# A graph layer on one core: columns copied by ScalarE alone, for 110 tiles instead of 298, with the edge attributes split in portions

## The chip, the cores and the metric

The kernel runs on one core of a Trainium2 chip. The core has TensorE (PE, matrix products), VectorE (DVE), ScalarE (ACT), GpSimd (POOL), the queue of SyncE (SP), which issues most transfers here, and 16 DMA engines that carry them out. GpSimd issues the gathers: one indirect DMA fetches 128 rows of a table in HBM, one row for each partition. The metric is the device time of one execution in microseconds (us). "Span" is the time from the first to the last instruction of the profiled execution.

## The reference, cut to what matters

N = 12500 nodes with 96 features, E = 412500 edges sorted by their target, 4 attributes to an edge.

```python
def _mlp(h, W, b, gamma, beta):
    h = relu(h @ W + b)
    mu, var = mean(h, axis=0), var(h, axis=0)
    return gamma * (h - mu) * rsqrt(var + EPS) + beta

node_feat = _mlp(x, W_node, ...)
edge_feat = _mlp(edge_attr, W_edge, ...)
message = concatenate([x[row], x[col], edge_feat], axis=1)
message = _mlp(message, W_msg, ...)
agg = segment_sum(message, col, num_segments=N)
x = layernorm(x + agg + node_feat)
```

The message's product falls into three: x[row] @ W1 + x[col] @ W2 + edge_feat @ W3. The first two are tables over nodes.

## The kernel before

**Units.** An edge tile is 128 edges (3223 of them), a group is 4 tiles = 512 edges (806 groups, `NG`), a block is 4 groups (202 blocks, `NBL`). Since the edges are sorted by target, a block's targets lie in a window of 31 nodes for each group.

**Tables and gathers.** `tables` writes `p_tab` = x @ W1 and `q_tab` = x @ W2 to HBM. `gather(g, pg)` lets GpSimd fetch the rows of `p_tab` for the sources of a group's tiles, one indirect DMA to a tile (L214). The groups of the first 4 blocks (`RAW`) are gathered from the input x instead, before `p_tab` is there. GpSimd is in use from the beginning: the generator `blocks` gathers the first 29 blocks (116 groups, `SPILL`) into a ring of 8 pairs of groups and stores them to HBM (`spill`, L239 to L241, on SP's queue). Block b's gathers need the ring slots of block b - 4; the spill store of block b - 2 is issued at the step at which the gathers of block b are. Every `next(store)` in the setup is such a step. `early_rows` fetches the last tile of three of these groups row by row on SP instead.

**Setup.** After the tables come: the targets relative to their blocks (`rel`) and a check; `split`, which splits the edge attributes into three bf16 parts (8 steps of 128 x 1792 elements: load x, ScalarE copies to bf16, VectorE subtracts, twice over, three stores to `stack_d`); `places`, which does the like for the targets' places; and then `edge_norm`, the statistics of the edge features. `edge_norm` loads `stack_d` in chunks of J = 8 blocks by `stacked` (three DMAs), multiplies (L425), applies Relu (L429, ScalarE) and takes statistics (L431, VectorE, `bn_stats`, 606 of them); at its end it aggregates them (L436), sums over the partitions with the matrix `pick` and makes the `bias` and the weight `w_e`. Between its chunks it steps `nodes` (the node features, L370 to L406), `early_rows` and `store`; what is left of these is drained behind it, `nodes` first.

**Main loop.** SP, GpSimd, PE, DVE and ACT follow an order written out by hand (`manual_schedule`). It runs over the 806 groups in the order of `plan`, which mixes the 116 spilled groups in among the 690 others. For a step k with group g: `message(k)` (L740, VectorE) adds the gathered rows to the product in PSUM and applies Relu; `squared` (L754, ScalarE) and `moments` (L760, VectorE) collect the squares; `places_of` (L748) marks each edge's target in its window, `sums` (L786, PE) adds the messages by target, `add` (L805, L806) adds the window to `agg`; `edges` (L704) and `prepare` (L712, ScalarE) make the edge features of the next block in `left`; `linear` (L720) multiplies them and the window's rows of `q_tab` (in `rhs`) for the step after the next. For a group past the spilled ones, `ahead_of(ahead)` then issues the gathers of the group 16 places further on, into the ring slots that this pair of groups has freed.

**Copied tiles.** For certain pairs of groups the last tile isn't gathered. Instead its 128 source columns are copied from x, which lies transposed in SBUF (`big`), into a tile `xc` of 96 x 128, one column to an instruction, with the column's place in a register; PE then multiplies `xc` by W1 (L725). `COPIED` lists the pairs: nine out of ten, 298 in all. Two `Stream`s share them, ScalarE's (L647, 24 columns to a step) and VectorE's (L645, 25 to a step on the mean, in the portions of `LOADS`); `load` reads the places into registers, `copy` issues the copies. `listed` fetches the places from HBM on SP's queue. In a slot whose tile isn't gathered, `ahead_of` has the place zeroed by VectorE (L506) unless it is zero already.

```python
COPIED = [q for q in range(RING // 2, LP - 6) if q % 10 != 10 - 1]
...
    a, b = to[:, 4 * (lo + i):4 * (lo + i + 1)], places_in_x[:, bass.ds(x - HOME, 4)]
```

**End.** Behind the last step come the statistics of the messages and `output`, the normed sum for all nodes.

Of the kernel before, what the change touches and what calls it, by code (L numbers as in the profile page):

```python
# [26 lines left out]
P = 128  # L27
# [12 lines left out]
NS = 3  # L40
RW = 7
NBQ = RW * 32
RL = NBQ * GE
NPL = 8
PART = 4
# [69 lines left out]
def gnn(ctx, tc, t):  # L115
# [10 lines left out]
    stack_d = dram.tile([HI + PLACES * BG, RL], BF16, name="stack_d")  # L126
# [126 lines left out]

    zero = const.tile([64, C], F32, name="zero")
# [52 lines left out]
    def split():  # L307

        with tc.tile_pool(name="sp", bufs=2) as work:
            n = RL // 8 // NPL  # L310
            rows = [stack_d[16 * i:16 * (i + 1), :].rearrange("r (c e) -> (r c) e", c=8) for i in range(3)]
            ea = t["ea"].rearrange("r (c b) e -> (r c) (b e)", c=8)
            made = []
            for k in range(NPL + 1):
                if k < NPL:
                    x = work.tile([P, n], F32, name="x")
                    nc.sync.dma_start(x, ea[:, k * n:(k + 1) * n])
                    y = [work.tile([P, n], BF16, name=f"y{i}") for i in range(3)]
                    nc.scalar.activation(y[0], x, AF.Copy)
                    nc.vector.tensor_sub(x, x, y[0])  # L320
                    nc.scalar.activation(y[1], x, AF.Copy)
                    nc.vector.tensor_sub(y[2], x, y[1])
                    made.append(y)
                if k:
                    for i in range(3):
                        nc.sync.dma_start(rows[i][:, (k - 1) * n:k * n], made[k - 1][i])
                if k % 3 == 2:
                    yield

    def places():  # L330

        with tc.tile_pool(name="lin", bufs=2) as work, tc.tile_pool(name="lin1", bufs=1) as one:
            first = one.tile([P, RW], I32, name="first")
            nc.sync.dma_start(first, t["first"])
            rows = [stack_d[HI + BG * i:HI + BG * (i + 1), :].rearrange("g (c b e) -> (g c) b e", b=RW, e=GE)
                    for i in range(PLACES)]
            parts = [slice(i, min(i + 2, RW)) for i in range(0, RW, 2)]
            made = []
            for i in range(len(parts) + 1):
                if i < len(parts):  # L340
                    n = parts[i].stop - parts[i].start
                    lin = work.tile([P, n, GE], I32, name="lin")
                    nc.sync.dma_start(lin, t["dlin"][:, parts[i], :])
                    rlin = work.tile([P, n, GE], F32, name="rlin")
                    nc.vector.tensor_tensor(rlin, lin, first[:, parts[i]].unsqueeze(2).to_broadcast([P, n, GE]),
                                            op=OP.subtract)
                    y = [work.tile([P, n, GE], BF16, name=f"z{i}") for i in range(PLACES)]
                    nc.scalar.activation(y[0], rlin, AF.Copy)
                    nc.scalar.activation(rlin, rlin, AF.Square)
                    nc.scalar.activation(y[1], rlin, AF.Copy)  # L350
                    nc.vector.tensor_sub(y[2], rlin, y[1])
                    made.append(y)
                if i:
                    for r, x in zip(rows, made[i - 1]):
                        nc.sync.dma_start(r[:, parts[i - 1], :], x)

    def stacked(to, b, n):

        cols = slice(b * GE, (b + n) * GE)
        for lo, hi, rows in ((16, 48, 32), (0, 16, 16), (HI, ON, HI + PLACES * BG)):  # L360
            nc.sync.dma_start(to[lo:hi], stack_d[:rows, cols].rearrange("r (b e) -> r b e", e=GE))
# [46 lines left out]
    def edge_norm(work, one, ps):  # L408
# [5 lines left out]
        for b in range(NBL):  # L414
# [6 lines left out]
            for i in range(NS):  # L421
                k = NS * b + i
                if k % 2 == 0:
                    pr = ps.tile([P, 2, GE], F32, name="pr")
                nc.tensor.matmul(pr[:, k % 2, :], wide[:, P * i:P * (i + 1)], ea[:, b % J, :],  # L425
                                 start=True, stop=True)
                if k % 2:
                    r = work.tile([P, 2, GE], F32, name="r", bufs=4)
                    nc.scalar.activation(r, pr, AF.Relu)  # L429
                    for o in (1, 0):  # L430
                        nc.vector.bn_stats(stats[:, (k - o) % NS, (k - o) // NS, :], r[:, 1 - o, :])  # L431

        part = one.tile([P, NS, 2], F32, name="part")
        square = one.tile([P, NS], F32, name="square")
        for i in range(NS):
            nc.vector.bn_aggr(part[:, i, :], stats[:, i, :, :].rearrange("p a b -> p (a b)"))  # L436
        nc.vector.tensor_mul(square, part[:, :, 0], part[:, :, 0])
        nc.vector.tensor_add(part[:, :, 1], part[:, :, 1], square)
        pick = one.tile([P, NS, C], F32, name="pick")
        nc.vector.memset(pick, 0.0)  # L440
        for i in range(NS):
            for o in range(-P * i % C - C, P, C):
                lo, hi = max(o, 0), min(o + C, P)
                if lo < hi:
                    to = pick[:, i, lo - o:hi - o]
                    nc.vector.tensor_add(to, to, ident[:, lo:hi])
        pm = ps.tile([C, 2], F32, name="pr")
# [3 lines left out]
        nc.vector.tensor_scalar(aggr, pm, float(NBL * GE) / E, None, op0=OP.mult)  # L451
# [5 lines left out]
        pb = ps.tile([1, C], F32, name="pr")  # L457
# [39 lines left out]
    def fast():  # L497
# [14 lines left out]
        with tc.manual_schedule(engines={ET.SP, ET.Pool}):  # L512
# [9 lines left out]
            with tc.tile_pool(name="nd", bufs=1) as nd, tc.tile_pool(name="nd_ps", bufs=2, space=PSUM) as nd_ps, \  # L522
                    tc.tile_pool(name="er", bufs=2) as er, tc.tile_pool(name="es", bufs=2) as es, \
                    tc.tile_pool(name="es1", bufs=1) as es1, tc.tile_pool(name="es_ps", bufs=3, space=PSUM) as es_ps:
                node, n, extra = nodes(nd, nd_ps), 7, early_rows(er)
                for i, _ in enumerate(edge_norm(es, es1, es_ps)):
                    next(node, None)
                    if i:
                        next(extra, None)
                    while 16 * i + 150 >= 20 * n:  # L530
                        next(store, None)
                        n += 1
                for x in (node, store, extra):
                    for _ in x:
                        pass
            got = {g: ahead_of(g) for g in range(SPILL, SPILL + RING)}
        with tc.tile_pool(name="fix", bufs=1) as fix, tc.tile_pool(name="msg", bufs=2) as work, \
                tc.tile_pool(name="msg_ps", bufs=2, space=PSUM) as ps:
            squares = fix.tile([P, C], F32, name="squares")
# [5 lines left out]
            by_place = [ps.tile([P, GE], F32, name=f"pa{i}", bufs=1) for i in range(2)]  # L545
# [10 lines left out]
            for x in left:  # L556
                nc.vector.memset(x[C:], 1.0)
# [4 lines left out]
            at = [fix.tile([P, BG, OW], F32, name=f"at{i}") for i in range(AB)]  # L562
            for x in at:
                nc.vector.memset(x, 0.0)
# [8 lines left out]
            late = [fix.tile([P, CL, GE], BF16, name=f"late{i}") for i in range(2)]  # L573
            early = fix.tile([P, CE, GE], BF16, name="early")
            for x in (*late, early):
                nc.vector.memset(x[C:], 1.0)

            def load(s):
# [17 lines left out]
                nc.sync.dma_start(rhs[C:C + WN, s % RB, :, :], rows)  # L596
# [24 lines left out]
            loaded = []  # L621

# [16 lines left out]
            def columns(j, lo, val, engine):  # L639

                to = xcs[j % XB].bitcast(U8)
                for i, x in enumerate(val):
                    a, b = to[:, 4 * (lo + i):4 * (lo + i + 1)], places_in_x[:, bass.ds(x - HOME, 4)]
                    if engine == ET.DVE:
                        nc.vector.tensor_copy(a, b)  # L645
                    else:
                        nc.scalar.activation(a, b, AF.Copy)  # L647
# [59 lines left out]
            def prepare(s, half):  # L707

                n = min(2, NG - order[s] * BG - 2 * half)
                if n > 0:  # L710
                    pr, x = prs.pop((s, half)), left[s % 2]
                    nc.scalar.activation(x[:C + WN, 2 * half:2 * half + n, :], pr[:C + WN, :n, :], AF.Relu)  # L712
# [44 lines left out]
            def moments(sq, at_last, stream=None):  # L757

                for i in range(2):
                    nc.vector.tensor_tensor(wide_sq, wide_sq, sq[:, i, :, :], op=OP.add)  # L760
                    if stream:
                        stream.load()
# [48 lines left out]
            with tc.manual_schedule(engines={ET.SP, ET.Pool, ET.PE, ET.DVE, ET.Activation}):  # L811
# [9 lines left out]
                prepare(1, 0)  # L821
                for k in range(ZB - 1):
# [3 lines left out]
                for k in range(last):  # L826
# [9 lines left out]
                    dves.load()  # L836
# [324 lines left out]
```

## Time and profile before

| | |
|---|---|
| runs shown | 3755.09, 3759.74, 3773.7 us (median 3759.74) |
| profiled execution, its own time | 3756.5 us |
| its span | 3754.8 us |
| HBM read, written | 243.91 MB, 56.09 MB |
| setup, up to the first L740 | 0 to 683 us |
| main loop and end | 683 to 3754.8 us |

A line of the costliest groups reads: line, engine, operation, out<-in with shapes, count | busy us, mean ns of one | idle time of the engine just before them and what ended it. "issue" means that nothing in the profile had to be waited for. A timeline's row reads: start in us, length, engine, line, operation, out<-in, count [idle time before <- what ended it]. Times and rows come from one profiled execution. In the rows for TensorE an operation may be missing; the rows of GpSimd's gathers are complete (2922).

### The profile page before, as it was taken

The page shows a single profiled execution, that of the slowest core. Times are in us where ns is not written, and L with a number is a line of the kernel's source. Part 1 is how long each engine was busy: PE and PEld are TensorE (multiplying, and loading weights), DVE is VectorE, ACT ScalarE, POOL GpSimd, SP SyncE. Part 2 cuts the span into 40 slices and gives each one's busy share as a digit, 9 for nine tenths or more (in the row PEclk, how much of TensorE's full clock was granted, in tenths as well). Part 3 has the DMA queues.
Part 4 walks back from the last instruction along what each step waited for, and adds up shares of the span by engine and source line. Part 5 has one row for each costly group of instructions (what it writes and reads, how often), then busy time and mean ns, then how long its engine had stood idle before and what let it go on. Part 6 is the DMA issues. An engine that isn't in the chain of part 4 may idle for free.

```text
span 3754.8 us, 85646 instructions
## 1 busy us (share of the span) xinstructions
PE 2529.5 (67%) x15765; PEld 2135.2 (57%) x15765; DVE 3048.1 (81%) x22677; ACT 2903.9 (77%) x19786; POOL 2805.0 (75%) x2950
## 2 busy tenths in 40 slices
PE   4335664677776777667777767777766767776766
PEld 4012231576666666656766666666665666666666
DVE  2489999788888888888888888888888888888864
ACT  1457885588888888888888888888888888888852
POOL 7777775777777777777777777777777777777776
PEclk7667786788888877887787787887888787788776
DMA  8764663222222222222222222222222222222233
GB/s 236 261 178 111 164 171 99 65 63 60 58 62 61 57 66 49 60 62 59 59 63 61 61 62 58 61 62 58 61 62 51 63 59 60 61 58 65 58 100 74
DMA packets 206325, 305.80 MB, mean 81 GB/s; under 512 B 121814, under 2 KB 128708, under 8 KB 202944
## 3 DMA queue, kind: packets, MB, share of 16 engines
q0 software_dynamic: 93504, 143.81, 18.8%
q1 hardware_dynamic: 99308, 151.50, 13.5%
q10 hardware_dynamic: 12960, 4.93, 0.5%
q14 instruction: 427, 3.50, 0.3%
q8 instruction: 126, 2.06, 0.2%
HBM read 243.91 MB, written 56.09 MB: 80 GB/s over the span
## 4 chain that ended last, share of the span: by engine, by line
DVE 50%; DMA 14%; issue 12%; POOL 12%; DVEq 9%; PE 1%; ACT 1%; SPq 0%; ACTq 0%; POOLq 0%
DVE xc L645 25%; POOL pg L214 12%; DMA pg<-p_tab,src 11%; DVE estats L431 9%; DVEq L634 9%; DVE mixed L760 7%; DVE h L740 4%; DMA q_tab<-trow 1%; DVE agg L806 1%; DMA x<-in_ea 1%; DVE at L748 1%; PE pt L198 1%; DMA cols<-in_lasts 0%; DVE nstats L372 0%; DVE agg L381 0%
## 5 line engine op out<-in xcount | busy, mean ns | idle before, releaser
L214 POOL DMA_INDIRECT pg<-p_tab,src x2858 | 2722.5, 953 | 903.1 <-issue 720.8
L647 ACT ACTIVATE xc<-big 96x4 uint8 x18560 | 1846.9, 191 | 208.0 <-issue 201.6
L720 PE MATMUL z<-rhs,left 128*128 128x96 f32 x6446 | 1157.1, 335 | 847.4 <-DVE h L740 829.7
L645 DVE COPY xc<-big 96x4 uint8 x19584 | 1540.7, 195 | 226.7 <-issue 220.4
L720 PEld LDWEIGHTS z<-rhs,left 128*128 128x128 f32 x6446 | 1018.4, 240 | 947.5 <-DVE h L740 925.3
L786 PEld LDWEIGHTS pa<-at,h 128*97 128x97 f32 x6446 | 839.6, 207 | 117.5 <-issue 50.6
L786 PE MATMUL pa<-at,h 128*97 128x80 f32 x6446 | 848.6, 287 | 3.3 <-DVE h L740 3.3
L754 ACT ACTIVATE sq<-h 128x768 f32<-128x768 f32 x404 | 338.1, 837 | 287.5 <-DVE h L740 282.8
L740 DVE CUSTOM_DVE_ANT_0 h<-z,pg 128x384 f32<-128x384 f32 x690 | 374.5, 543 | 193.6 <-DMA pg<-p_tab,src 185.1
L760 DVE TENSOR_TENSOR mixed<-mixed,sq 128x384 f32<-128x384 f32 x802 | 448.6, 559 | 53.5 <-DVE h L740 18.4
L712 ACT ACTIVATE left<-pr 127x1024 f32<-127x1024 f32 x403 | 403.5, 1001 | 39.7 <-PE pr L704 39.7
L429 ACT ACTIVATE r<-pr 128x1024 f32<-128x1024 f32 x303 | 306.7, 1024 | 99.1 <-DVE estats L431 73.1
L425 PE MATMUL pr<-ea,wide 128*128 128x512 bf16 x606 | 225.2, 466 | 223.0 <-ACT r L429 146.8
L431 DVE BATCH_NORM_STATS2 estats<-r 128x6 f32<-128x512 f32 x606 | 361.0, 675 | 5.3 <-ACT r L429 5.3
L704 PE MATMUL pr<-late,we 128*128 128x512 bf16 x690 | 279.4, 497 | 17.7 <-DVE at L748 15.4
L425 PEld LDWEIGHTS <-wide 128*128 128x128 bf16 x606 | 67.4, 112 | 355.6 <-issue 257.6
L748 DVE TENSOR_TENSOR at<-rel,mixed 128x496 f32<-128x496 bf16 x202 | 132.3, 655 | 4.9 <-DVE h L740 4.6
L725 PE MATMUL z<-w_msg,xc 96*128 96x96 f32 x596 | 131.6, 307 | 0.0
L704 PEld LDWEIGHTS <-we 128*128 128x128 bf16 x806 | 109.6, 140 | 21.1 <-issue 19.5
L725 PEld LDWEIGHTS z<-w_msg,xc 96*128 96x128 f32 x596 | 107.1, 224 | 0.0
L805 DVE TENSOR_TENSOR total<-pa,total 97x1 f32<-97x1 f32 x202 | 31.8, 157 | 57.0 <-issue 45.8
L214 POOL DMA_INDIRECT pg<-in_x,src_raw x64 | 60.7, 949 | 20.6 <-issue 19.2
(132 smaller groups left out, 803.9 us busy)
## 6 DMA issues: line engine op xcount, KB each, us to landing
pg<-p_tab,src POOLq DMA_INDIRECT x2858
pb<-spill SPq DMA_DIRECT2D x29, 768.0 KB
spill<-pg SPq DMA_DIRECT2D x55, 384.0 KB
ea<-stack_d SPq DMA_DIRECT2D x25, 480.0 KB
stack_d<-y SPq DMA_DIRECT2D x24, 448.0 KB
late<-stack_d SPq DMA_DIRECT2D x57, 180.0 KB
rhs<-q_tab SPq DMA_DIRECT2D x202, 46.5 KB
x<-in_ea SPq DMA_DIRECT2D x8, 896.0 KB
```

The lines of the kernel that those rows point to most:

```text
L214: made = [nc.gpsimd.indirect_dma_start(out=pg[:, i, :], out_offset=None, in_=tab[:, :], in_offset=bass.IndirectOffsetOnAxis(ap=idx[:, i:i ...
L431: nc.vector.bn_stats(stats[:, (k - o) % NS, (k - o) // NS, :], r[:, 1 - o, :])
L634: _, val = nc.values_load_multi_w_load_instructions(numbers[q // TURN % 2][:, q % TURN, lo:hi], engines=[engine], min_val=HOME, max_val=HO ...
L645: nc.vector.tensor_copy(a, b)
L647: nc.scalar.activation(a, b, AF.Copy)
L704: nc.tensor.matmul(prs[s, half][:, i, :], we[:, 2 * half + i, :], block[s], start=True, stop=True)
L712: nc.scalar.activation(x[:C + WN, 2 * half:2 * half + n, :], pr[:C + WN, :n, :], AF.Relu)
L720: nc.tensor.matmul(zb[k % ZB][:, i * C:(i + 1) * C], left[s % 2][:KR, g % BG, i * P:(i + 1) * P], rhs[:KR, s % RB, g % BG, :], start=True, ...
L740: nc.vector._custom_dve(TENSOR_ADD_SAT, out=h[:, :n, :], in0=z, in1=rows[:, :n, :], s0=MOST, s1=0.0)
L754: nc.scalar.activation(sq[:, :m, :n, :], hb[k // 2 % HP][:, k % 2:k % 2 + m, :n, :C], AF.Square)
L760: nc.vector.tensor_tensor(wide_sq, wide_sq, sq[:, i, :, :], op=OP.add)
L786: nc.tensor.matmul(by_place[s % 2][:C + 1, :NW], hb[k // 2 % HP][:r, k % 2, t, :], at[s % AB][:r, i, o + NW * t:o + NW * (t + 1)], start=i ...
```

## The change

- `COPIED` lists every third pair (q % 3 == 1), 110 tiles, and `LOADS` gives all columns to ScalarE, 20 to a step; VectorE's stream is empty. The copy is of one f32 column rather than four bytes. (`columns` has a new form for VectorE, which isn't used with these `LOADS`.)
- `split` and `places` become one generator, `stacking`: 16 steps of 128 x 896 attributes, on every other step with one eighth of the places (112 x 512). `stack_d` is cut into 8 portions of 28 blocks. Four steps stand ahead of `edge_norm`, the others between its chunks, which are of 7 blocks now. The drain behind it takes `store` first and `nodes` last.
- `edge_norm` ends with sums over the statistics in place of L436 (a Square on ScalarE, three reductions and one more operation on VectorE); the rest of its end is `edge_bias`, called at the head of the main loop's section, behind first writes by ScalarE of the rows of ones and VectorE's zeroing of one `at`. `pick` is made earlier.
- The bias is written into `rhs` in one ScalarE instruction, at row C instead of the last row, in place of 12 DMAs; the weights in `wp` are turned to match, so that `prepare` covers all 128 rows and `left` needs no ones.
- In the main loop VectorE's places for reading registers are one in place of four.

```diff
-LOADS = (((24,),) * 4, ((8, 8, 12), (20,), (8, 8, 12), (12, 12)))
+LOADS = (((20,),) * 4, ((),) * 4)
-COPIED = [q for q in range(RING // 2, LP - 6) if q % 10 != 10 - 1]
+COPIED = [q for q in range(RING // 2, LP - 6) if q % 3 == 1]
-J = 8
+J = 7
-    stack_d = dram.tile([HI + PLACES * BG, RL], BF16, name="stack_d")
+    stack_d = [dram.tile([HI + PLACES * BG, PB * GE], BF16, name=f"stack{i}") for i in range(NPT)]
...
+    def stacking(one, work):
+        first = one.tile([BG * PB, NPT], I32, name="first")
+        nc.sync.dma_start(first, t["first"])
+        n = PB * GE // 8 // 2
+        made = []
+        def stored():
+            for to, x in made:
+                nc.sync.dma_start(to, x)
+            made.clear()
+        for u in range(2 * NPT):
+            p, half = u // 2, slice(u % 2 * n, (u % 2 + 1) * n)
+            x = work.tile([P, n], F32, name="x")
+            nc.sync.dma_start(x, t["ea_by_part"][p][:, half])
+            if u % 2 == 0:
+                lin = one.tile([BG * PB, GE], I32, name="lin")
+                nc.sync.dma_start(lin, t["dlin"][p])
+            stored()
+            y = [work.tile([P, n], BF16, name=f"y{i}") for i in range(3)]
+            nc.scalar.activation(y[0], x, AF.Copy)
+            nc.vector.tensor_sub(x, x, y[0])
+            nc.scalar.activation(y[1], x, AF.Copy)
+            nc.vector.tensor_sub(y[2], x, y[1])
+            made += [(stack_d[p][16 * i:16 * (i + 1), :].rearrange("r (c e) -> (r c) e", c=8)[:, half], y[i])
+                     for i in range(3)]
+            if u % 2 == 0:
+                rlin = one.tile([BG * PB, GE], F32, name="rlin")
+                nc.vector.tensor_tensor(rlin, lin, first[:, p:p + 1].to_broadcast([BG * PB, GE]), op=OP.subtract)
+                z = [one.tile([BG * PB, GE], BF16, name=f"z{i}") for i in range(PLACES)]
+                nc.scalar.activation(z[0], rlin, AF.Copy)
+                nc.scalar.activation(rlin, rlin, AF.Square)
+                nc.scalar.activation(z[1], rlin, AF.Copy)
+                nc.vector.tensor_sub(z[2], rlin, z[1])
+                made += [(stack_d[p][HI + BG * i:HI + BG * (i + 1), :].rearrange("g (c e) -> (g c) e", e=GE), z[i])
+                         for i in range(PLACES)]
+            yield
+        stored()
...
-        for i in range(NS):
-            nc.vector.bn_aggr(part[:, i, :], stats[:, i, :, :].rearrange("p a b -> p (a b)"))
...
+        nc.scalar.activation(squared, means, AF.Square)
+        nc.vector.tensor_reduce(two[:, :, 0:1], rest, axis=AX.X, op=OP.add)
+        nc.vector.tensor_reduce(part[:, :, 0:1], means, axis=AX.X, op=OP.add)
+        nc.vector.tensor_reduce(two[:, :, 1:2], squared, axis=AX.X, op=OP.add)
...
-            for _ in split():
-                next(store)
-            places()
-            for i in range(2):
-                next(store)
...
-                node, n, extra = nodes(nd, nd_ps), 7, early_rows(er)
+                node, stack, n, extra = nodes(nd, nd_ps), stacking(st1, st), 5, early_rows(er)
+                for _ in range(4):
+                    next(stack)
                 for i, _ in enumerate(edge_norm(es, es1, es_ps)):
+                    if i % 2:
+                        next(stack, None)
                     next(node, None)
-                    if i:
+                    if i > 2:
                         next(extra, None)
-                    while 16 * i + 150 >= 20 * n:
+                    while 18 * i + 95 >= 20 * (n - 1):
                         next(store, None)
                         n += 1
-                for x in (node, store, extra):
+                for x in (store, extra, node):
...
-            for i in range(RB):
-                for k in range(BG):
-                    nc.sync.dma_start(rhs[KR - 1:KR, i, k, :], bias)
...
+                nc.scalar.activation(rhs[C:C + 1], bias[:, None, None, :].to_broadcast([1, RB, BG, C]), AF.Copy)
...
-                        nc.scalar.activation(a, b, AF.Copy)
+                        nc.scalar.activation(to[:, lo + i:lo + i + 1], x.bitcast(F32), AF.Copy)
...
-                    nc.scalar.activation(x[:C + WN, 2 * half:2 * half + n, :], pr[:C + WN, :n, :], AF.Relu)
+                    nc.scalar.activation(x[:, 2 * half:2 * half + n, :], pr[:, :n, :], AF.Relu)
```

More of the change, by code (lines that the diff above doesn't have):

```diff
@@ L252, in gnn @@
                 next(store)
+    const_part = const.tile([P, NS, 2], F32, name="part")
+    pick = const.tile([P, NS, C], F32, name="pick")
+    nc.vector.memset(pick, 0.0)
+    for i in range(NS):
+        for o in range(-P * i % C - C, P, C):
+            lo, hi = max(o, 0), min(o + C, P)
+            if lo < hi:
+                to = pick[:, i, lo - o:hi - o]
+                nc.vector.tensor_add(to, to, ident[:, lo:hi])
     zero = const.tile([64, C], F32, name="zero")
@@ L305, in gnn @@
         nc.vector.tensor_scalar(flag, most, 0.0, None, op0=OP.is_gt)
[L307 to L352, printed above, removed]
-                if i:
-                    for r, x in zip(rows, made[i - 1]):
-                        nc.sync.dma_start(r[:, parts[i - 1], :], x)
@@ L363, in nodes @@
+    def stacked(to, b, n):
+        while n:
+            p, o = b // PB, b % PB
+            m = min(n, PB - o)
+            for lo, hi, rows in ((16, 48, 32), (0, 16, 16), (HI, ON, HI + PLACES * BG)):
+                nc.sync.dma_start(to[lo:hi, :m], stack_d[p][:rows, o * GE:(o + m) * GE].rearrange("r (b e) -> r b e", e=GE))
+            to, b, n = to[:, m:], b + m, n - m
     def nodes(one, ps):
@@ L427, in edge_norm @@
                 if k % 2:
-                    r = work.tile([P, 2, GE], F32, name="r", bufs=4)
+                    r = work.tile([P, 2, GE], F32, name="r", bufs=3)
                     nc.scalar.activation(r, pr, AF.Relu)
@@ L431, in edge_norm, with edge_bias @@
                         nc.vector.bn_stats(stats[:, (k - o) % NS, (k - o) // NS, :], r[:, 1 - o, :])
-        part = one.tile([P, NS, 2], F32, name="part")
-        square = one.tile([P, NS], F32, name="square")
-        for i in range(NS):
[L436 to L447, printed above, removed]
+        part = const_part
+        n = NBL * 2
+        means, rest = (stats.rearrange("p i b (h s) -> p i (b h) s", s=3)[:, :, :, o] for o in (1, 2))
+        squared = eas[0].rearrange("p j e -> p (j e)").bitcast(F32)[:, :NS * n].rearrange("p (i n) -> p i n", i=NS)
+        nc.scalar.activation(squared, means, AF.Square)
+        two = one.tile([P, NS, 2], F32, name="two")
+        nc.vector.tensor_reduce(two[:, :, 0:1], rest, axis=AX.X, op=OP.add)
+        nc.vector.tensor_reduce(part[:, :, 0:1], means, axis=AX.X, op=OP.add)
+        nc.vector.tensor_reduce(two[:, :, 1:2], squared, axis=AX.X, op=OP.add)
+        nc.vector.scalar_tensor_tensor(part[:, :, 1:2], two[:, :, 0:1], 2.0 / GE, two[:, :, 1:2], op0=OP.mult, op1=OP.add)
+    def edge_bias(one, pm, pb):
+        part = const_part
         for i in range(NS):
@@ L538, in fast @@
                 tc.tile_pool(name="msg_ps", bufs=2, space=PSUM) as ps:
+            late = [fix.tile([P, CL, GE], BF16, name=f"late{i}") for i in range(2)]
+            early = fix.tile([P, CE, GE], BF16, name="early")
+            for x in (*late, early):
+                nc.scalar.activation(x[C:], eps[C:, :, None].to_broadcast([P - C, x.shape[1], GE]), AF.Copy,
+                                     scale=0.0, bias=1.0)
+            at = [fix.tile([P, BG, OW], F32, name=f"at{i}") for i in range(AB)]
+            nc.vector.memset(at[0], 0.0)
+            by_place = [ps.tile([P, GE], F32, name=f"pa{i}", bufs=1) for i in range(2)]
+            edge_bias(fix, by_place[0][:C, :2], by_place[1][:1, :C])
             squares = fix.tile([P, C], F32, name="squares")
@@ L560, in fast @@
                 nc.vector.memset(x[:, :, :, C:], 1.0)
-            at = [fix.tile([P, BG, OW], F32, name=f"at{i}") for i in range(AB)]
             for x in at:
-                nc.vector.memset(x, 0.0)
+                if x is not at[0]:
+                    nc.vector.memset(x, 0.0)
                 for i in range(BG):
@@ L572, in fast @@
             eas, block, prs, windows = {}, {}, {}, {}
[L573 to L576, printed above, removed]
             def load(s):
@@ L595, in load @@
                 rows = bass.AP(rows.tensor, rows.offset, [[C, WN], [WS * C, BG], [1, C]], None, rows.runtime_checks)
-                nc.sync.dma_start(rhs[C:C + WN, s % RB, :, :], rows)
+                nc.sync.dma_start(rhs[C + 1:KR, s % RB, :, :], rows)
                 block[s] = ea
@@ L639, in columns @@
             def columns(j, lo, val, engine):
[L641 to L647, printed above, removed]
+                to = xcs[j % XB]
+                of = [places_in_x[:, bass.ds(x.with_bounds(guaranteed_mod_val=0, out_of_modulus=4) - HOME, 4)] for x in val]
+                if engine == ET.DVE:
+                    to = to.bitcast(I32)
+                    for i in range(0, len(val), 2):
+                        a, b = (x.bitcast(I32) for x in of[i:i + 2])
+                        nc.vector.scalar_tensor_tensor(to[:, lo + i:lo + i + 2], first_of_two, a, b.to_broadcast([C, 2]),
+                                                       op0=OP.bitwise_and, op1=OP.bitwise_xor)
+                    if lo + len(val) == P:
+                        pairs = to.rearrange("c (e two) -> c e two", two=2)
+                        nc.vector.tensor_tensor(pairs[:, :, 0], pairs[:, :, 0], pairs[:, :, 1], op=OP.bitwise_xor)
+                else:
+                    for i, x in enumerate(of):
+                        nc.scalar.activation(to[:, lo + i:lo + i + 1], x.bitcast(F32), AF.Copy)
             class Stream:
```

48 lines of the change are left out of this document (21 added, 27 removed).

## The prediction

> **What bounds the kernel now.** I read the page first: the span, the busy shares, the slices, the chain of waits and the costliest groups.
>
> ```profile
> span 3754.8 us, 85646 instructions
> PE 2529.5 (67%) x15765; PEld 2135.2 (57%) x15765; DVE 3048.1 (81%) x22677; ACT 2903.9 (77%) x19786; POOL 2805.0 (75%) x2950
> DVE  2489999788888888888888888888888888888864
> POOL 7777775777777777777777777777777777777776
> DVE 50%; DMA 14%; issue 12%; POOL 12%; DVEq 9%; PE 1%; ACT 1%; SPq 0%; ACTq 0%; POOLq 0%
> L214 POOL DMA_INDIRECT pg<-p_tab,src x2858 | 2722.5, 953 | 903.1 <-issue 720.8
> L647 ACT ACTIVATE xc<-big 96x4 uint8 x18560 | 1846.9, 191 | 208.0 <-issue 201.6
> L645 DVE COPY xc<-big 96x4 uint8 x19584 | 1540.7, 195 | 226.7 <-issue 220.4
> L740 DVE CUSTOM_DVE_ANT_0 h<-z,pg 128x384 f32<-128x384 f32 x690 | 374.5, 543 | 193.6 <-DMA pg<-p_tab,src 185.1
> L214 POOL DMA_INDIRECT pg<-in_x,src_raw x64 | 60.7, 949 | 20.6 <-issue 19.2
> ```
>
> VectorE has the highest busy share and half of the chain, and half of its work is L645, which the change removes. That reading misleads. GpSimd's digit is 7 in all slices but two, setup and main loop alike, and its pauses are put down to "issue", that is, to nothing that the profile shows. And L740, which consumes the gathered rows, waits almost only for their DMA. So I looked at single gathers in GpSimd's timeline (start, length, line, and idle before). The pairs of rows below begin and end runs of 153, 2409 and 55 gathers; the first row shown is the first gather of all.
>
> ```profile
> 3.03 1.12 POOL L214 DMA_INDIRECT pg<-in_x,src_raw  x1 [1.42 <-DMA src_raw<-in_src]
> ...
> 400.03 0.94 POOL L214 DMA_INDIRECT pg<-p_tab,src  x1 [0.30 <-issue]
> ...
> 589.81 0.94 POOL L214 DMA_INDIRECT pg<-p_tab,src  x1 [0.30 <-issue]
> ...
> 700.48 0.94 POOL L214 DMA_INDIRECT pg<-p_tab,src  x1 [0.30 <-issue]
> ...
> 3640.24 0.94 POOL L214 DMA_INDIRECT pg<-p_tab,src  x1 [0.30 <-issue]
> ...
> 3707.64 0.94 POOL L214 DMA_INDIRECT pg<-p_tab,src  x1 [0.30 <-issue]
> ```
>
> From 400.03 to 589.81 there are 152 steps: 1.2486 us each. From 700.48 to 3707.64 there are 2408: 1.2488 us each. From 3640.24 to 3707.64 there are 54: 1.2481 us each. The pitch is 0.94 of work and 0.30 between, always. Who copies columns in these stretches? The windows of L645 alone answer (stretch, length, VectorE's busy time in that line and its count, granted clock, DMA share, GB/s):
>
> ```profile
> 330.00:600.00 270.00, 0.00 (x0) 0.80 0.61 155
> 700.00:3600.00 2900.00, 1515.03 (x19257) 0.80 0.27 60
> 3640.00:3708.00 68.00, 0.00 (x0) 0.58 0.35 91
> ```
>
> With no VectorE copy and with 19,257 of them the pitch is the same. So GpSimd issues gathers back to back from 3.0 to 3708.9 us, and the span is the number of gathers times 1.2488, plus pauses S. In numbers: 3.0 before the first, 2922 gathers (2858 + 64) x 1.2488 = 3649.0, and 3754.8 - 3708.9 = 45.9 after the last, together 3697.9; S is the remaining 56.9. **The bound is GpSimd.** S has three parts in the rows:
>
> ```profile
> 135.65 0.94 POOL L214 DMA_INDIRECT pg<-p_tab,src  x1 [6.84 <-DMA spill<-pg]
> 635.57 0.94 POOL L214 DMA_INDIRECT pg<-p_tab,src  x1 [24.84 <-DMA spill<-pg]
> 622.06 0.34 SPq L389 DMA_DIRECT2D y_d<-y0s  x1
> 630.58 2.22 SPq L241 DMA_DIRECT2D spill<-pg  x4
> 116.00:208.00 92.00, 68.79 (x53) 0.60 0.81 279
> 294.28 4.37 DVE L381 SCALAR_TENSOR_TENSOR agg<-agg,norm_node,big 96x1250 f32<-96x1250 f32 x3
> 296.92 1.13 POOL L214 DMA_INDIRECT pg<-p_tab,src  x1 [0.30 <-issue]
> ```
>
> Two waits for ring slots whose spill store was late (6.8 and 24.8; the second because SP stood before the node store L389 until 622.1), and gathers that ran longer: in 116 to 208 us, the split's stretch (a window's row of GpSimd, columns as above), 53 gathers took 68.8 us, 18.8 over 53 x 0.944. The last two rows show the same lengthening while VectorE runs L381, an operation with two SBUF inputs.
>
> **The change, part by part.**
>
> Gathers. A tile whose columns are copied isn't gathered. The kernel has 3223 tiles, of which 3 are fetched singly by SP and 298 copied (18560/128 = 145 by ScalarE, 19584/128 = 153 by VectorE): 2922 gathers, as counted. The new list takes q = 10, 13, ..., 337, that is 110 tiles, so 3223 - 3 - 110 = 3110 gathers, 188 more. At 1.2488: **+234.8 us**, all on the bounding engine.
>
> VectorE's copies. 1540.7 us of busy time go, off the path: VectorE waits for gathered rows today. What could they be worth? Only a lower pitch, and that is 1.2486 without copies against 1.2488 with them: 3110 x 0.0002 = 0.6 us. I take nothing.
>
> A rule of the Trainium skill speaks against my sum. Its page "SBUF — State Buffer", section "Who interferes with whom", says that a VectorE copy in a two-port mode holds the port pair that GpSimd shares, and GpSimd then blocks; this would make removing the copies a gain of GpSimd's time. By that rule the main loop's pitch should lie above the copy-free stretches; the trace doesn't agree, at 1.2488 against 1.2486 and 1.2481. The same section's other rule, that an operation with two SBUF inputs contends with a GpSimd instruction that reads SBUF, agrees with the 1.13 us gathers beside L381.
>
> ScalarE's copies. 14080 instead of 18560, now of one f32 column, not four bytes; no row has that form. Nearest is L647: 1846.9/18560 = 0.0995 us each in a row of them, 0.191 alone. I take 0.0995 (the element count falls, nothing else is known): 20 per step give 1.99 us, and these rows of the main loop add the rest:
>
> ```profile
> L712 ACT ACTIVATE left<-pr 127x1024 f32<-127x1024 f32 x387 | 387.3, 1001 | 2.8 <-PE pr L704 2.8
> L754 ACT ACTIVATE sq<-h 128x768 f32<-128x768 f32 x388 | 325.4, 839 | 218.4 <-DVE h L740 217.2
> ```
>
> Both come about every second step: 0.50 + 0.42. ScalarE needs 2.9 us a step. GpSimd's step is (3110 - 525) x 1.2488 / 806 = 4.0 us (525 gathers lie ahead of the loop: 461 spilled, 64 of the ring). Hidden, with 1.1 us to spare; a tile comes every 7 steps, 140 columns at 20 a step against 128 needed. VectorE keeps L740, L748, L760 and the adds, under 1.5 us a step. The zeroing of an ungathered tile's place (L506) comes up to 110 times, 0.14 us each by its row, also under that cover.
>
> Setup. The split's 8 wide steps become 16 half-width ones, of which 4 stand before the edge statistics and 12 among them. SP has each step's loads, three stores (six on every other step) and now three `stacked` loads for 7 blocks rather than 8, in one queue with the spill stores. The new waits are SP's, on y and z of the split; behind them stand x, ea and the spill stores, and for those GpSimd waits. I price three things.
>
> (a) Lengthening of gathers beside two-input VectorE work.
>
> ```profile
> L320 DVE TENSOR_TENSOR x<-x,y 128x1792 f32<-128x1792 f32 x8 | 16.2, 2024 | 31.3 <-ACT y L319 31.3
> L351 DVE TENSOR_TENSOR z<-rlin,z 128x1024 bf16<-128x1024 f32 (+1 forms) x4 | 4.4, 1091 | 5.4 <-ACT z L350 5.4
> 206.38 0.69 DVE L351 TENSOR_TENSOR z<-rlin,z 128x512 bf16<-128x512 f32 x1 [0.61 <-ACT z L350]
> ```
>
> Today 16 x 2.02 + 8 x 1.09 = 41 us of it cost 18.8. The new 896-wide subtraction lies between 0.69 and 2.02; about 1.1 by interpolation: 32 x 1.1 + 16 x 0.69 = 46 us, so 21; with L381 and one long gather at the start, 26. Bounds: 10 to 30.
>
> (b) The early slot wait. The 97th gather needs the spill of block 2. That store now stands behind four split steps and the first statistics loads: I estimate its issue at 133 us instead of 125, so 12 of waiting instead of 6.8. Bounds: 0 to 40.
>
> (c) The late slot wait, 24.8. Spill stores are drained ahead of the node work and the node steps end some chunks before the statistics. I take it as gone; bound 0 to 25.
>
> S becomes about 39 (26 + 12 + 1 for the start) instead of 57: **-18 us**.
>
> Does the setup then end in time? GpSimd can run ahead until 3.0 + 525 x 1.2488 + 39 = 698 us, when it needs the first messages done. The statistics are VectorE's:
>
> ```profile
> L431 DVE BATCH_NORM_STATS2 estats<-r 128x6 f32<-128x512 f32 x606 | 361.0, 675 | 5.3 <-ACT r L429 5.3
> 219.34 8.40 DVE L372 BATCH_NORM_STATS2 nstats<-agg 96x6 f32<-96x512 f32 x14
> 639.76 16.58 DVE L436 BATCH_NORM_AGGREGATE part<-estats 128x2 f32<-128x1212 f32 x3
> 682.93 0.56 DVE L740 CUSTOM_DVE_ANT_0 h<-z,pg 128x384 f32<-128x384 f32 x1 [7.42 <-PE z L720]
> ```
>
> Today they run from 219 to 640, 421 us with the node work; 12 split steps add about 35. Begun at 140 they end near 596, and the first message follows about 30 later (43 today, less the 16.6 of L436, which few-microsecond reductions replace, and without the bias's stores to `rhs`). That is 626, some 70 us early. Everything else in the setup (bias in place, ones rows by ScalarE, `pick` made earlier) lies under that cover.
>
> **Sum:** 3.0 + 3110 x 1.2488 + 39 + 45.9 = 3971.7 us of span, against 3754.8. The profiled execution took 3756.5, the median of the runs shown is 3759.7; adding 2 to 3 us gives **3974 us**, 5.7% slower.
>
> **The rivals.**
>
> *The pitch falls (faster).* If VectorE's copies hold something that GpSimd needs, gathers speed up once they go. Each 0.01 us of pitch is 31 us. To be level with before, the pitch must reach (3754.8 - 48.9 - 39) / 3110 = 1.179; 0.5% faster begins at 1.173; were the whole 0.30 gap to go, 3110 x 0.944 + 88 = 3024. For it: 0.30 between gathers has no releaser. Against: three stretches with and without copies within 0.0007 us. Chance 0.03.
>
> *The setup becomes the bound.* Begins when the first message comes after 698, that is when the statistics pass takes over 528 us; 29 chunks at 20 us each make 580, 140 + 580 + 30 = 750, and 52 us more: 4026. For it: SP's one queue and the waits in it. Against: 70 us of room. Chance 0.06.
>
> *ScalarE becomes the bound.* From (4.0 - 0.92) / 20 = 0.154 us a column; at the full 0.191 a step costs 4.74, over 704 copying steps 0.74 x 704 = 520 more: about 4490. Against: 0.0995 in the nearest row. Chance 0.02.
>
> *It doesn't do what it says:* no tile is copied at all, 3220 x 1.2488 + 88 = 4109. Chance 0.01.
>
> **How the numbers follow.** My case has 0.88. Its own range: S from 12 (no waits, 10 of lengthening) to 75 gives 3947 to 4010; I give 3945 to 4010, which leaves out the four rivals and a little of my case, under 0.2 together. A measurement of this kernel can tell about 0.5% from no change: 19 us. Faster by over that needs the first rival in full: 0.02; within it 0.01; slower 0.97.
>
> **What would show it.** Right: 3046 + 64 gathers in two L214 groups, single gathers still 0.94 + 0.30 apart, GpSimd's last gather near 3926, VectorE's busy time down to some 1500 us, a slot wait near 130 us, none near 610, the first L740 before 698. Wrong: a pitch clearly under 1.2488 in the main loop; a long GpSimd wait for VectorE or a spill after 600 us; ScalarE over 90% busy with `xc`.

## The result and the profile after

The kernel after takes 3983.56 us (median of 4 runs, 3975.45 to 3992.81), before 3766.39 (4 runs, 3755.09 to 3773.7): 1.0572 times as long, 95% interval 1.0545 to 1.06. Forecast were 3974 us, 3945 to 4010. In both kernels the executions fall into two groups some 17 us apart (3755 to 3760 and 3773 to 3774; 3975 to 3976 and 3991 to 3993); the profile before is of a short one, the profile after of a long one, with the difference wholly behind the last gather, as the last section shows.

The page after, in the order of the lines shown of before:

```profile
span 3991.1 us, 59044 instructions
PE 2668.7 (67%) x15169; PEld 2272.8 (57%) x15389; DVE 1564.5 (39%) x3183; ACT 2459.6 (62%) x15339; POOL 2988.3 (75%) x3138
DVE  3899884333333332333333333332233333333323
POOL 7677777777777777777777777777777777777774
POOL 42%; issue 26%; DMA 20%; DVE 7%; PE 4%; ACT 1%; SPq 0%; POOLq 0%; ACTq 0%; DVEq 0%; another core or an unknown queue 0%
L212 POOL DMA_INDIRECT pg<-p_tab,src x3046 | 2905.3, 954 | 938.7 <-issue 843.4
L654 ACT ACTIVATE xc<-big 96x1 f32 x14080 | 1382.1, 190 | 124.7 <-issue 119.3
L747 DVE CUSTOM_DVE_ANT_0 h<-z,pg 128x384 f32<-128x384 f32 x690 | 384.8, 558 | 2204.6 <-DMA pg<-p_tab,src 2131.1
```

VectorE's digit falls from 8 to 3 in the main loop, GpSimd's stays at 7, and the kernel is longer. The chain now names GpSimd and its gaps (42% and 26%); VectorE waits 2131 us for gathered rows. That is the bound of before, seen more plainly because VectorE is no longer busy beside it. GpSimd's timeline after (the first gather, one with a wait, one that is long, two that bound the copying part of the main loop with 2323 gathers from the one to the other, and the last):

```profile
3.23 1.12 POOL L212 DMA_INDIRECT pg<-in_x,src_raw  x1 [1.61 <-DMA src_raw<-in_src]
...
139.28 0.94 POOL L212 DMA_INDIRECT pg<-p_tab,src  x1 [10.53 <-DMA spill<-pg]
...
520.23 14.03 POOL L212 DMA_INDIRECT pg<-p_tab,src  x1 [0.30 <-issue]
...
700.93 0.94 POOL L212 DMA_INDIRECT pg<-p_tab,src  x1 [0.30 <-issue]
...
3599.65 0.94 POOL L212 DMA_INDIRECT pg<-p_tab,src  x1 [0.30 <-issue]
...
3926.71 0.94 POOL L212 DMA_INDIRECT pg<-p_tab,src  x1 [0.30 <-issue]
```

From 700.93 to 3599.65 there are 2322 steps of 1.24837 us (1.24882 before). From the first gather to the last it is 3926.71 - 3.23 = 3109 x 1.24837 + 42.3, so S is 42. Before, in the same terms, it was 2921 x 1.24882 + 56.8. The last gather comes 219.1 us later: +233.4 for number and pitch, -14.5 for the pauses, +0.2 for the start.

### The profile page after: what moved, and what is told of

Its sections match the earlier page's. It is cut to its first block, busy times and chain, and to the rows that moved or that the text cites. A ratio compares the mean times of both kernels' runs of the same rounds, so it can differ in the third digit from the quotient of the medians.

```text
span 3991.1 us, 59044 instructions
## 1 busy us (share of the span) xinstructions
PE 2668.7 (67%) x15169; PEld 2272.8 (57%) x15389; DVE 1564.5 (39%) x3183; ACT 2459.6 (62%) x15339; POOL 2988.3 (75%) x3138
## 3 DMA queue, kind: packets, MB, share of 16 engines
q0 software_dynamic: 99520, 153.06, 18.9%
## 4 chain that ended last, share of the span: by engine, by line
POOL 42%; issue 26%; DMA 20%; DVE 7%; PE 4%; ACT 1%; SPq 0%; POOLq 0%; ACTq 0%; DVEq 0%; another core or an unknown queue 0%
POOL pg L212 42%; DMA pg<-p_tab,src 16%; DVE estats L431 5%; PE py L1084 1%; DVE mixed L767 1%; PE z L727 1%; DVE h L747 1%; DMA y_d<-y0s 1%; DMA q_tab<-trow 1%; PE pt L196 0%; PE pn L398 0%; DMA cols<-in_lasts 0%; PE pn L370 0%; DMA ea<-stack 0%; DMA p_tab<-trow 0%
## 5 line engine op out<-in xcount | busy, mean ns | idle before, releaser
L212 POOL DMA_INDIRECT pg<-p_tab,src x3046 | 2905.3, 954 | 938.7 <-issue 843.4
L727 PE MATMUL z<-rhs,left 128*128 128x96 f32 x6446 | 1249.1, 354 | 926.6 <-DVE h L747 921.5
L727 PEld LDWEIGHTS z<-rhs,left 128*128 128x128 f32 x6446 | 1107.2, 258 | 1020.1 <-DVE h L747 1014.0
L654 ACT ACTIVATE xc<-big 96x1 f32 x14080 | 1382.1, 190 | 124.7 <-issue 119.3
L791 PEld LDWEIGHTS pa<-at,h 128*97 128x97 f32 x6446 | 912.8, 223 | 132.2 <-issue 65.1
L791 PE MATMUL pa<-at,h 128*97 128x80 f32 x6446 | 918.1, 303 | 32.9 <-issue 22.4
L719 ACT ACTIVATE left<-pr 128x1024 f32<-128x1024 f32 x403 | 405.8, 1007 | 97.6 <-PE pr L711 47.7
L429 ACT ACTIVATE r<-pr 128x1024 f32<-128x1024 f32 x303 | 303.4, 1024 | 103.1 <-PE pr L425 57.2
L711 PE MATMUL pr<-late,we 128*128 128x512 bf16 x515 | 238.5, 526 | 58.4 <-ACT left L719 57.9
L747 DVE CUSTOM_DVE_ANT_0 h<-z,pb 128x384 f32<-128x384 f32 x100 | 52.4, 545 | 18.9 <-PE z L727 18.9
L732 PE MATMUL z<-w_msg,xc 96*128 96x96 f32 x220 | 52.4, 328 | 0.0
```

The source lines that it names most:

```text
L212: made = [nc.gpsimd.indirect_dma_start(out=pg[:, i, :], out_offset=None, in_=tab[:, :], in_offset=bass.IndirectOffsetOnAxis(ap=idx[:, i:i ...
L654: nc.scalar.activation(to[:, lo + i:lo + i + 1], x.bitcast(F32), AF.Copy)
L711: nc.tensor.matmul(prs[s, half][:, i, :], we[:, 2 * half + i, :], block[s], start=True, stop=True)
L719: nc.scalar.activation(x[:, 2 * half:2 * half + n, :], pr[:, :n, :], AF.Relu)
L727: nc.tensor.matmul(zb[k % ZB][:, i * C:(i + 1) * C], left[s % 2][:KR, g % BG, i * P:(i + 1) * P], rhs[:KR, s % RB, g % BG, :], start=True, ...
L747: nc.vector._custom_dve(TENSOR_ADD_SAT, out=h[:, :n, :], in0=z, in1=rows[:, :n, :], s0=MOST, s1=0.0)
```

## The experiments

Theory G: the span is the number of gathers, each at GpSimd's pitch, plus pauses in the setup. Rivals: S, the new setup costs the time; V, VectorE's copies hold up the gathers.

**Four runs that can't tell the theories apart.** The first four kernels (the new list alone, the rest of the change alone, VectorE as the copier, 55 tiles) ran when the kernel before itself took 5167.53 us (median of 15); later the same chip took 3755 for it, in one execution. The new list alone, the rest alone and 55 tiles ran again and stand further below; VectorE as the copier of the 110 tiles, in this form, ran only here:

```diff
-LOADS = (((20,),) * 4, ((),) * 4)
+LOADS = (((),) * 4, ((20,),) * 4)
...
+                        nc.vector.tensor_copy(to.bitcast(U8)[:, 4 * (lo + i):4 * (lo + i + 1)],
+                                              places_in_x[:, bass.ds(x - HOME, 4)])
```

> The kernel after with its 110 tiles copied by VectorE alone (four bytes to a column, as before) instead of ScalarE. Theory G: the same 3110 gathers, last gather at 3.1 + 3109 x 1.2488 + 43.5 = 3929 us, within 3 us of the kernel after (3926.7), though VectorE is busy by some 1100 us more. Rival V: gathers lengthen or their pitch rises clearly above 1.2488 while VectorE copies.

The four took 5146.58 to 5210.84 us, within 1.2% of each other though they have 2922 to 3165 gathers. ScalarE's timeline in the copies-alone kernel, at 3018 us, shows why they tell nothing of the theories:

```profile
3018.09 0.20 ACT L647 ACTIVATE xc<-big 96x4 uint8 x1 [0.52 <-issue]
3018.80 0.20 ACT L647 ACTIVATE xc<-big 96x4 uint8 x1 [0.50 <-issue]
3019.52 0.20 ACT L647 ACTIVATE xc<-big 96x4 uint8 x1 [0.52 <-issue]
```

One copy every 0.71 us in this stretch, where 18 of them took 1.99 us at 3010 us, 0.11 each, and nothing in the profile that it waited for. GpSimd waited for VectorE's messages in the main loop (901 us in 200 waits for L740), so that neither theory could show, and the expectation above is neither met nor refuted. That the engines got their instructions late would fit these gaps; it wasn't tested.

**The new list alone** (before, with `COPIED` and `LOADS` of after and nothing else):

> The run e1_copies_alone once more, on a chip where the kernel before takes its usual time: the kernel before with the new list of 110 copied tiles alone. Theory G (GpSimd issues gathers back to back at 1.2485 us): old pauses of 57 us, last gather at 3.1 + 3109 x 1.2485 + 57 = 3942 us, time about +235 on before. Rival S (the rearranged setup costs the time): last gather near 3708. Rival V (VectorE's copies hold something that gathers need): last gather well under 3942.

```profile
636.00 0.94 POOL L214 DMA_INDIRECT pg<-p_tab,src  x1 [24.97 <-DMA spill<-pg]
...
3942.10 0.94 POOL L214 DMA_INDIRECT pg<-p_tab,src  x1 [0.30 <-issue]
```

The last gather comes at 3942.1, forecast 3942. The time is 4008.09 us, 1.0654 times before (1.0619 to 1.069). The old late slot wait is there, so this part alone costs 234 us to the last gather. S and V fall: the setup is the old one, and taking 19,584 copies from VectorE left the pitch at 1.2485.

**The rest of the change alone** (after, with the old list, the old portions and VectorE's old copies put back):

> The run e2_setup_alone once more, on a chip where the kernel before takes its usual time: the kernel after with the old list of 298 tiles and the old copies put back. Theory G: 2922 gathers, pauses of 43.5 us: last gather at 3.1 + 2921 x 1.2488 + 43.5 = 3694 us, 13 to 14 before that of the kernel before. Rival S: at or behind 3708.

```profile
3693.58 0.94 POOL L212 DMA_INDIRECT pg<-p_tab,src  x1 [0.30 <-issue]
```

3693.6, forecast 3694: 14.1 us ahead of before (3707.6). The time is 0.9971 times before (0.995 to 0.9992); the lowest of each are 3740.99 and 3755.31. So the new setup gains 14.1 us, the list loses 234.5, and the two together, 220, are within 2 us of the 219 of the whole.

**55 tiles** (`q % 6 == 1`), on a chip where the kernel before took 3761.72 us at the least:

> The run e4_55_tiles once more, on a chip where the kernel before takes its usual time: every sixth pair (55 tiles) copied. Theory G: 3165 gathers, 55 x 1.2485 = 69 us behind the kernel after, last gather at 3995. Rival (the copies cost the bound as much as they save): under 30 us more than after.

The last gather came at 4002.6, not 3995. That chip's pitch in the main loop was 1.2507; 3164 x 1.2507 + 3.2 + 42 = 4002, so the count holds and the pitch is the chip's. Its lowest time, 4050.16, is 288.4 over its before; by G 243 gathers x 1.2507 = 303.9 less the setup's 14 is 290. The copies cost the bound no more than the 2 us between these two.

**The gather of 14 us.** In the kernel after, one gather at 520 us takes 14.03 instead of 0.94. VectorE beside it:

```profile
518.62 0.68 DVE L431 BATCH_NORM_STATS2 estats<-r 128x6 f32<-128x512 f32 x1
521.88 10.62 DVE L406 MEMSET agg<- 97x12672 f32 x1 [2.59 <-PE pr L425]
532.42 1.03 DVE L336 TENSOR_TENSOR x<-x,y 128x896 f32<-128x896 f32 x1
```

The gather ends at 534.26, 0.81 after L336, the split's subtraction with two SBUF inputs. In the kernel before the same zeroing had statistics behind it, and the gathers beside it (597 to 608 us) took 0.94. Theory Q: a two-input operation that stands in line behind another already keeps GpSimd out. A gather of 13.98 to 14.67 us stands beside the zeroing in all seven traces with the subtraction behind it (three of the first four kernels among them), and in none of the three that have gathers beside the zeroing on VectorE but something else behind it. Two kernels separate the subtraction from the zeroing itself. One zeroes on ScalarE:

```diff
-        nc.vector.memset(agg, 0.0)
+        nc.scalar.activation(agg, eps[:C + 1].to_broadcast([C + 1, WT]), AF.Copy, scale=0.0)
```

> The kernel after with the zeroing of agg at the end of the node work (12672 elements a partition, recorded as 10.6 us on VectorE) moved to ScalarE. In the kernel after one gather, begun at 520.2, took 14.0 us instead of 0.94 while VectorE zeroed agg with the split's two-input subtraction queued next. Theory Q (a two-input operation of VectorE that waits in line behind a running one already keeps GpSimd from reading, until 0.8 us after its end): without the long operation in front no gather is over 4 us after 200 us into the kernel; the long one falls to 2 us or less, 12 us gained if GpSimd is the bound. Rival E (that gather met the single-row fetches which SP issued from 518 to 525 us, or the zeroing itself shuts GpSimd out): a gather of 10 us and more stays near the same place in the order.

The rows of the gathers from 200 us on (shortest, median, longest in ns, first and last start), after and here:

```profile
L212 POOL DMA_INDIRECT pg<-p_tab,src x2968: 940/944/14027, 199.4 to 3926.7; - x198
```

```profile
L212 POOL DMA_INDIRECT pg<-p_tab,src x2966: 940/944/1828, 199.7 to 3911.9; - x198
```

The long gather is gone, and the last gather comes 14.8 us earlier (the early slot wait was also 2 us shorter). This kernel was executed once, in 3977.95 us. The other kernel leaves the zeroing on VectorE and puts the split's steps on the even chunks (`if i % 2 == 0`):

> The kernel after with the split's steps on the even chunks of the edge statistics instead of the odd ones; the zeroing of agg stays on VectorE. Theory Q (the 14 us gather is held by the split's two-input subtraction that stands in line behind the zeroing): the zeroing now has statistics behind it, not a subtraction, so no gather is over 4 us after 200 us, and the last gather comes some 12 us before that of the kernel after, at 3914. Rival Z (in the new setup the zeroing on VectorE itself shuts GpSimd out): one gather of 10 us and more stays, last gather near 3927.

VectorE and one of the gathers beside it:

```profile
517.12 10.62 DVE L406 MEMSET agg<- 97x12672 f32 x1 [3.47 <-PE pr L425]
527.65 0.29 DVE L400 COPY y0s<-pn 128x192 f32<-128x192 f32 x1
```

```profile
519.96 0.95 POOL L212 DMA_INDIRECT pg<-p_tab,src  x1 [0.30 <-issue]
```

With a copy behind the zeroing all gathers beside it are normal, the longest after 200 us is 1.88 us. Z falls, and so does E: here the single-row fetches are issued from 523.8 to 529.8 us, and the gathers beside them take 0.95 too. This kernel ran on the chip with the pitch of 1.2507, so its last gather at 3925.6 isn't to be set against 3914: 3.4 + 3109 x 1.2507 leaves 34 of pauses instead of 42: 13 less for the long gather, 3 more for the early slot wait (13.7), and some 1 more of other lengthening. Its median time is 3974.6 us, 1.0557 times before there (1.0512 to 1.0602).

**Two columns to an instruction on VectorE** (after, with `LOADS` of the diff for VectorE as the copier, and the change's own form of the copy), meant to show Q in the main loop:

> The kernel after with its 110 tiles copied by VectorE alone in the new form that the change brings but doesn't use: two columns to an instruction, from two inputs in SBUF. Gathers stay 3110. Theory Q (a two-input operation of VectorE, running or queued, keeps a gather from reading until it has ended): some 10 such instructions in a row at each of 704 steps, so a gather that begins among them is held to the end of the row: the mean gather rises from 0.954 by 0.05 to 0.25 us, the kernel by 150 to 800 us. Rival (only the number of gathers counts, whoever copies): within 5 us of the kernel after.

```profile
L647 DVE SCALAR_TENSOR_TENSOR xc<-first_of_two,big 96x2 int32<-96x2 int32 x7040 | 1009.0, 211 | 454.7 <-issue 443.3
L212 POOL DMA_INDIRECT pg<-p_tab,src x3046 | 2905.5, 954 | 939.0 <-issue 738.9
```

A miss: the mean gather is 954 ns as in after, the pitch 1.2486, the last gather 3927.2 against 3926.7, the time 3984.31 us against 3983.56. 7040 two-input operations of 2 elements, in rows of ten, lengthen no gather of the main loop by more than 0.05 us. So what I made of Q, that a gather waits for the whole row, is wrong. What stands is that a long two-input operation holds a gather until it has ended: in the kernel after, 36 of the 38 gathers of over 1 us end 0.81 to 0.84 us behind the end of such an operation. That the hold can begin before the operation starts, when something long is in front of it, rests on this one place in the kernel. As a result of its own, this run shows that VectorE can copy the 110 tiles in ScalarE's place, in this form, at the same time: only the count matters.

**What the theories point to.** The new setup, the old 298 copies, zeroing on ScalarE, and one spill store earlier:

```diff
-                for _ in range(4):
+                for i in range(4):
                     next(stack)
+                    if i == 1:
+                        next(store)
+                        n += 1
```

> What theories G and Q point to: the new setup, the old 298 copies by both engines, the zeroing of agg on ScalarE, and one spill store earlier, after the second of the four split steps. Theory G with Q: 2922 gathers, the pauses fall from 43.5 by 12.8 (zeroing) and some 6 to 10 (early slot wait): last gather at 3.1 + 2921 x 1.2488 + 23 = 3674 us, 34 before that of the kernel before, time 0.5 to 1% under it. Rival: VectorE or ScalarE becomes the bound once GpSimd is ahead, last gather stays at 3694 or behind.

```profile
151.85 0.94 POOL L212 DMA_INDIRECT pg<-p_tab,src  x1 [2.76 <-DMA spill<-pg]
...
3673.86 0.94 POOL L212 DMA_INDIRECT pg<-p_tab,src  x1 [0.30 <-issue]
```

3673.9, forecast 3674. The time is 3722.65 us, 0.9911 times before (0.9876 to 0.9947). Then 17 tiles more (`q % 20 != 19`, ScalarE 28 columns a step, VectorE 26):

> The best version so far (e8_best) with 315 tiles copied instead of 298, ScalarE 28 columns a step, VectorE 26. Theory G: 17 gathers fewer, 21 us: last gather at 3653. Where it ends: ScalarE needs 28 x 0.097 + 0.92 = 3.64 us a step and GpSimd's step falls to 3.69, so the room is nearly used up; if ScalarE's or VectorE's share is the bound in stretches, GpSimd shows waits for DVE over 0.3 us and the last gather comes later than 3653, up to that of e8_best (3674) or behind.

```profile
3659.09 0.95 POOL L212 DMA_INDIRECT pg<-p_tab,src  x1 [0.30 <-issue]
700.00:3500.00 2800.00, 2012.98 (x13298) 1834.38 (x13487) 2347.40 (x20618) 2527.54 (x20696) 2117.58 (x2238) 0.79 0.23 60
```

The second row is a window: length, then the busy times of PE, PEld, DVE, ACT and POOL. After the early wait of 2.5 us no gather has more than the usual 0.30 to 0.32 us in front of it, so GpSimd is still the bound, with ScalarE at 90% (2527.54 of 2800). On this chip of pitch 1.2511 the last gather at 3659 is what 2905 gathers and 23 of pauses make. So the forecast of 3653 missed by the chip's pitch, and ScalarE's room did not run out. The time is 0.986 times before (0.9816 to 0.9904), the lowest ratio of all: its lowest is 3703.44, before's there 3761.72, 58 less; for the version with 298 tiles it was 35 less (3720.40 against 3755.31).

## Why the prediction was right, step by step

- *The bound.* GpSimd's pitch, not VectorE's half of the chain: held with 55, 110, 298 and 315 tiles copied.
- *188 gathers at 1.2488, +234.8.* 3110 gathers, +233.4 with the change in pitch; alone, 234.5 to the last gather.
- *VectorE's copies worth nothing.* The pitch fell from 1.24882 to 1.24837, 1.4 us over 3110 gathers; 0.6 was said.
- *The rule against the sum.* The Trainium skill (page "SBUF — State Buffer", section "Who interferes with whom") has VectorE's copies in a two-port mode shut GpSimd out. The runs show no such loss for these copies of 4 bytes: taking 19,584 away and putting them back left the pitch between 1.2484 and 1.2488. Whether the copies ran in such a mode no trace shows. But the two do meet, which the prediction overlooked, and it is the copy that waits. In the trace of before, from 700 to 3600 us, 1289 gathers have the end of a VectorE copy in their last 0.2 us, and 1267 of these end within 9 ns behind it; that copy is recorded with 0.40 us (median), the others with 0.16. The gathers themselves hardly wait: 944.5 ns on the mean, 943.5 where no such copy is near. So taking the copies away freed VectorE, and GpSimd had little to gain. The section's rule for two-input operations agrees for long ones; for 2 elements no gather was longer by more than 0.05 us.
- *ScalarE hidden.* 1382.1/14080 = 0.0982 us a column (0.0995 taken), 62% busy.
- *(a) Lengthening, 26.* 32.0, of which 13.1 is the one gather behind the zeroing; the others make 18.9. That the size came near is luck: the one gather was not foreseen, and without it 26 would have been 7 too much.
- *(b) Early slot wait, 12.* 10.5 idle, 10.2 over the usual gap.
- *(c) Late slot wait gone.* Gone; in the copies-alone kernel it stayed, 24.97.
- *Setup in time.* The first message came at 642.5, 626 was said. The statistics ran from 145 to 622, where 140 to 596 was said: VectorE waited 28 us for ScalarE's Relu (L429, 5 before), and I had taken it as always busy. The message followed 20 us later, not 30. With room to 698 all this cost nothing.
- *The end, 45.9.* The term that was mis-sized for the profiled execution: 3991.1 - 3928.0 = 63.1. The executions of 3975.45 and 3975.95 us weren't profiled; they are shorter by the 17 that lie between 63 and the 46 of the sum.

Of the rivals none occurred: the pitch didn't fall by more than 0.0005, the setup wasn't late, ScalarE had room, and the columns were copied (14080 = 110 x 128).

## What to carry to other kernels

An engine that repeats one short operation at an unvarying pitch, with a gap that the profile calls "issue", can be the bound at 75% busy; test it by comparing its pitch in stretches where the suspected other engine is idle. Copies that look like VectorE's burden were here payment for a gather less on GpSimd: 1.25 us for 128 columns' copying on engines that had room. Price a change by the bounding engine's count first, and its pauses next.

## What was not expected of the hardware

The output's products (L1084 after, L1079 before) took 42.1 us in the profile after and 22.1 before, in windows of 43 and 22 us; the columns behind the five busy times are the granted clock, the DMA share and GB/s:

```profile
3938.00:3981.00 43.00, 42.48 (x199) 42.00 (x197) 22.58 (x35) 12.45 (x22) 14.29 (x10) 0.50 0.31 83
```

```profile
3719.00:3741.00 22.00, 21.71 (x194) 21.71 (x195) 18.57 (x30) 10.92 (x19) 11.60 (x8) 1.00 0.45 120
```

TensorE was granted half its speed there in the one and all of it in the other. Of the ten profiles of executions under 4100 us, after, the zeroing on ScalarE, the new list alone, the rest alone and the last version had 42.1, the other five 22.1, so it isn't the change; what decides it stays open. In these ten, 63 to 64 us lie behind the last gather with the one and 46 with the other. That fits the 17 us between executions of one kernel; executions without a profile can't show it.

A two-input operation of VectorE in line behind a 10.6 us zeroing held a gather for 13 us, while short ones by the thousand held none by more than 0.05 us. The gather began 1.65 us ahead of the zeroing's recorded start (1.6 to 2.3 in the seven traces), so either that start is recorded late or the hold began earlier still; that wasn't settled. Nor does any run show what fills the 0.30 us between two gathers; theory G needs only that it doesn't vary.
